# Keys and values of two groups by seven products in one PSUM bank, in an attention layer on one core

## The chip, the cores and the metric

The kernel runs on one core of a Trainium2 chip. The metric is the time of one execution on the device in microseconds; smaller is better. A core has a matrix engine (TensorE, in profiles PE, with its weight loads as PEld), a vector engine (VectorE, DVE), an activation engine (ScalarE, ACT), a general engine (GpSimd, POOL) and a queue engine (SyncE, SP) that issues most of the DMAs. Each has its own in-order queue, and they wait for each other by semaphores. Matrix products land in PSUM, which has eight banks of 2 KB in each of 128 partitions; everything else lies in SBUF.

## The reference

All numbers are float32. For x of 2 batches x 512 tokens x 512 features, with 32 query heads in 8 groups (four query heads share one key head and one value head of 128 columns):

```python
q = x @ Wq + bq;  k = x @ Wk + bk;  v = x @ Wv + bv        # 4096, 1024 and 1024 columns
q, k = rope(q, pos), rope(k, pos)
scores = einsum("bgrsd,bgtd->bgrst", q, k) / sqrt(128)     # masked to t <= s
ctx = einsum("bgrst,bgtd->bgrsd", softmax(scores), v)
x = layernorm(x + ctx @ Wo + bo)
# then a dense layer with four low-rank experts, mixed by a softmaxed router
y = x @ W_base.T + b_base + sum_e alpha_e * (x @ A_e.T @ B_e.T) * 2
out = layernorm(x + y)
```

Four experts of sixteen are active; their rows of lora_A, lora_B and router_W are gathered by index.

## The kernel before

**Units, parts, slots.** A *unit* is one group of one batch: 16 units. Units 0 to 11 go through groups 0 to 5 with both batches each; the last four are (6,0), (7,0), (6,1), (7,1). A unit has four *parts* (128 query tokens of its four heads) and a part four *slots*; a slot is the softmax of 128 rows (32 tokens x 4 heads) over the keys up to the diagonal, so its width grows from 32 to 512 columns within a unit. `slot(T)` writes down the work of slot T for all engines by hand: the schedule is manual, so each engine executes in the order in which the code issues. `put(n, f)` appends f to the end of slot n.

**The softmax chain.** In slot T: `score(T)` on PE (L488), then `masked_max(T-1)` on DVE (L496), `exponentials(T-1)` and `normalise(T-3)` on ACT (L503, L511), `blocks_transposed(T-4)` on DVE (L519, L521). When four slots are done, `blocks_out` writes the part's weights to DRAM and `blocks_in` reads them back transposed as pT (L529, L537, on SP). `weigh` (L544) multiplies pT with v on PE, 12 slots after the part's first score and later, and `context_out` (L550) copies the bank to SBUF on ACT. Score banks are two, the context bank is one.

**Projections.** x is held transposed as xT. Keys: four products of 128x512 per unit (`k_mm`, `proj_mm`, L355), one in each of the first four slots of the unit before. Then `k_rope` in three steps on DVE (L368, L371, L375) and one on POOL (L376) straight from the bank. Values: `v_mm` (L342) makes a tile of 128 tokens x 256 columns, both groups of a pair, by four products; `v_out` (L347) adds bv, broadcast over the partitions, on DVE. Two such tiles fall into each unit.

Queries are already made by Strassen's scheme in Winograd's form, two heads at a time and a batch halved into twice 256 tokens: seven products of half the size instead of eight (`q_products`, `product`, L429, two matmuls of 256 columns each). Sums of the weights are made on POOL (`w_sums`, `strassen_sums`, L416 to L419), sums of x once per batch on DVE (`x_sums`, xs). The products go to two banks, qx and qy; after certain products ACT copies the running sum of qx (`q_copy`, L457, L460), and DVE adds qy to the copy (`q_sum`, L467 to L472).

Wo is multiplied in the same way (`wo_products`, `ctx_sums` on POOL, `wo_sums` on DVE, L568), in slots that begin 21 after a unit's first (`wo_from`); its results are added to x on DVE (`wo_adds`, L601).

**What sets the order of loads.** SP takes its DMAs in order, and one that waits holds the next. `load_q`, `load_k`, `load_wv` and `load_wo` are put into slots by hand; each waits until its buffer is free.

Of the kernel before, what the change touches and what calls it, by code (L numbers as in the profile page):

```python
# [29 lines left out]
def postln_layer_kernel(  # L30
# [84 lines left out]
    rope_sb = const.tile([P, 2, S], F32, name="rope_sb")  # L115
    bqkT = const.tile([P, H + G], F32, name="bqkT")

# [43 lines left out]
    def load_wv(gg):  # L161
        wv_g = wts.tile([P, KC, VN], F32, tag="wv_g", name=f"wv_{gg}", bufs=1)
        nc.sync.dma_start(out=wv_g, in_=Wv[:, ts(gg, VN)].rearrange("(c p) n -> p c n", p=P))
        bv_g = wts.tile([P, VN], F32, tag="bv_g", name=f"bv_{gg}")
        nc.sync.dma_start(out=bv_g, in_=bv[ts(gg, VN)].partition_broadcast(P))
        wvs[gg] = wv_g, bv_g

# [20 lines left out]

    bqk = setup.tile([H + G, D], F32, name="bqk")
    nc.scalar.dma_start(out=bqk[:H, :], in_=bq.rearrange("(h d) -> h d", d=D))  # L190
    nc.scalar.dma_start(out=bqk[H:, :], in_=bk.rearrange("(h d) -> h d", d=D))
    for t in range(TPB):
# [25 lines left out]
    nc.gpsimd.iota(lane, pattern=[[0, 1]], base=0, channel_multiplier=1)  # L218
    a_act = setup.tile([EAR, HID], F32, name="a_act")
    r_act = setup.tile([EA, HID], F32, name="r_act")  # L220
    rb_act = setup.tile([EA, 1], F32, name="rb_act")
# [41 lines left out]
    def gather_experts():  # L263
        gather(a_act, lora_A.rearrange("e r n -> (e r) n"), idx["a"])
        gather(r_act, router_W, idx["e"])
        for a in range(EA):
            gather(b_act[:, a, :], lora_B.rearrange("e (p j) r -> (e p) (j r)", j=BJ), idx["b"][:, a : a + 1])
# [11 lines left out]
    def lora_weights(step):  # L279
        if step == 0:  # L280
            ta = ps_wo.tile([P, KC, EAR], F32, tag="wx", name="ta")
            for c in range(KC):
                nc.tensor.transpose(ta[:, c, :], a_act[:, ts(c, P)], ident[:EAR, :EAR])
            nc.vector.tensor_copy(arT[:, :, :EAR], ta)
            nc.vector.tensor_copy(b_jar, b_act.rearrange("p a (j r) -> p j a r", r=RK))
        elif step == 1:
            tr = ps_wo.tile([P, KC, EA], F32, tag="wx", name="tr")
            for c in range(KC):
                nc.tensor.transpose(tr[:, c, :], r_act[:, ts(c, P)], ident[:EA, :EA])
            nc.vector.tensor_copy(arT[:, :, EAR:], tr)  # L290
        else:

            tbm = ps_wo.tile([EAR, BJ, P], F32, tag="wx", name="tbm")
            for j in range(BJ):
                nc.tensor.transpose(tbm[:, j, :], b_jar[:, j, :, :].rearrange("p a r -> p (a r)"), ident)
            nc.vector.tensor_copy(bmT[:EAR, :].rearrange("k (p j) -> k j p", j=BJ), tbm)
# [41 lines left out]
    def v_mm(gg, t, c, pool, tag):  # L338

        if c == 0:  # L340
            psq["v", gg, t] = pool.tile([P, VN], F32, tag=tag, name="pv")
        nc.tensor.matmul(  # L342
            psq["v", gg, t], lhsT=xT[:, c, ts(t, P)], rhs=wvs[gg][0][:, c, :], start=(c == 0), stop=(c == KC - 1))

    def v_out(gg, t):
        v_sb[gg, t] = work.tile([P, VN], F32, tag="v", name=f"v_{gg}_{t}", bufs=11)
        nc.vector.tensor_tensor(v_sb[gg, t], psq["v", gg, t], wvs[gg][1], ALU.add)  # L347

# [9 lines left out]
    def rope_step(key, bias_col, part, dst):  # L358
# [8 lines left out]
        if part == 0:  # L367
            nc.vector.scalar_tensor_tensor(  # L368
                t2[lo, :], q[hi, :], b_ap[hi, :], rope_sb[hi, 1, :], ALU.add, ALU.mult)
        elif part == 1:  # L370
            nc.vector.scalar_tensor_tensor(  # L371
                t2[hi, :], q[lo, :], b_ap[lo, :], rope_sb[lo, 1, :], ALU.add, ALU.mult)
        else:
            t1 = proj.tile([P, S], F32, tag="raw0", name="t1", bufs=2) if key in in_psum else q
            nc.vector.scalar_tensor_tensor(t1, q, b_ap, rope_sb[:, 0, :], ALU.add, ALU.mult)  # L375
            nc.gpsimd.tensor_tensor(  # L376
                dst, t1[:].rearrange("p (n s) -> p n s", s=BLK), t2[:].rearrange("p (n s) -> p n s", s=BLK), ALU.add)

    def k_mm(u, c):
        g, b = unit(u)  # L380
        proj_mm(("k", u), ps_k, "k", wqk["k", g], slice(0, D), b, c)

    def k_rope(u, part):
        if part == 0:
            kT[u] = work.tile([P, UNIT, BLK], F32, tag="kT", name=f"kT_{u}")
        rope_step(("k", u), H + unit(u)[0], part, kT[u])
# [46 lines left out]
    def q_products(u, k, step):  # L433
# [18 lines left out]
        else:  # L452
            product(halves[key]["qy"], w[:, 2], x2[:, :, TH:], False)

    def q_copy(u, k, name):
        if name == "c21":
            nc.scalar.copy(psq["q", u, 2 * k + 1][:, :TH], halves[u, k]["qx"])  # L457
            return
        part = halves[u, k][name] = proj.tile([P, TH], F32, tag=name, name=name)
        nc.scalar.copy(part, halves[u, k]["qx"])  # L460

    def q_sum(u, k, step):
        key = u, k
        z = halves[key]
        if step == 0:
            psq["q", u, 2 * k] = proj.tile([P, S], F32, tag="raw0", name="q0", bufs=2)
            nc.vector.tensor_tensor(psq["q", u, 2 * k][:, :TH], z["qy"], z["p1"], ALU.add)  # L467
        elif step == 2:
            psq["q", u, 2 * k + 1] = proj.tile([P, S], F32, tag="raw1", name="q1")
            nc.vector.tensor_tensor(psq["q", u, 2 * k + 1][:, TH:], z["qy"], z["u3"], ALU.add)  # L470
        else:
            nc.vector.tensor_tensor(psq["q", u, 2 * k][:, TH:], z["qy"], z["u2"], ALU.add)  # L472

# [65 lines left out]
    def weigh(p, j):  # L539
        u, i = parts[p]  # L540
        g, b = unit(u)
        if j == 0:
            psc[p] = ps_ctx.tile([P, R, P], F32, tag="ctx", name="pc")
        nc.tensor.matmul(  # L544
            psc[p], lhsT=v_sb[g // VG, b * TPB + j][:, ts(g % VG, D)], rhs=pT[p][:, :, ts(j, P)],
            start=(j == 0), stop=(j == i))

    def context_out(p):
        ctxT[p] = work.tile([P, R, P], F32, tag="ctxT", name=f"ctxT_{p}", bufs=3)
        nc.scalar.copy(ctxT[p], psc[p])  # L550

# [241 lines left out]
    put(T_BEGIN, gather_experts)  # L793
    for n, gg, t in [(2 * t - 1, 0, TPB + t) for t in range(TPB)] + [(2 * t + 11, 1, t) for t in range(3)]:
        put(n, lambda gg=gg, t=t: v_tile(gg, t, ps_wo, "wx"))
        put(n + 1, lambda gg=gg, t=t: v_out(gg, t))
# [3 lines left out]
    for k in range(3):  # L800
        put(-4 + k, lambda k=k: prior_weights(k))
        put(12 + 2 * k, lambda k=k: lora_weights(k))
    put(1, lambda: load_q(1, 1))
    put(6, lambda: load_wv(1))
    put(9, lambda: load_wo(1))
    for t in range(NT):
# [7 lines left out]
    for m, (n, k) in enumerate(pairs):  # L814
        if n:
            put(q_from(set_units(n)[0], k) - 9, lambda n=n, k=k: w_sums(n, k))
        if m > 3:
            before, k_before = pairs[m - 3]
            put(q_from(set_units(before)[-1], k_before) + 8, lambda n=n, k=k: load_q(n, k))
    for g in range(2, G):  # L820
        put(2 * UNIT * (g - 1) - 24, lambda g=g: load_k(g))
    for gg in range(2, G // VG):
        put(4 * UNIT * (gg - 1) + 30, lambda gg=gg: load_wv(gg))

# [5 lines left out]
    for n in range(NSETS - 2):  # L830
        for k in range(4):
            put(wo_from(set_units(n)[0]) - 1 + k, lambda n=n, k=k: wo_sums(n, k))

# [15 lines left out]
    def slot(T):  # L849
# [13 lines left out]
        uk, l = divmod(T + UNIT, UNIT)  # L863
        if 0 < uk < NU and l < KC:
            k_mm(uk, l)

        gv, tv = divmod(2 * (uk - 3) + (l >= 11), NT)
        gv += 1
        new_v = 0 < gv < G // VG and (gv > 1 or tv >= 3)
        if new_v and l in (7, 8, 11, 12):  # L870
            for c in range(2):
                v_mm(gv, tv, 2 * (l in (8, 12)) + c, ps_k, "k")
        kw, sw = divmod(T - LAG_WO, 8)
# [13 lines left out]
        if now and step in (0, 2, 4, 6):  # L887
            q_copy(uq, kq, ("p1", "u2", "u3", "c21")[step // 2])
        for part, j in weigh_at.get(T - 1, ()):
            if j == parts[part][1]:  # L890
# [11 lines left out]
        if now and step in (1, 5, 7):  # L902
            q_sum(uq, kq, {1: 0, 5: 2, 7: 3}[step])
        if 0 <= T - 2 < T_END:
# [15 lines left out]
        if 0 <= r < R and part < 3:  # L920
            q_rope(1, r, part)
        if 0 < uk < NU and l in (KC, KC + 1, KC + 2):
            k_rope(uk, l - KC)
        if new_v and l in (10, 14):
            v_out(gv, tv)
        if plain and step_o:
# [12 lines left out]
    for t in range(TPB):  # L939
        transpose_token_tile(xT[:, :, ts(t, P)], x_sb[:, t, :], *spare[t], copies[t % 2])  # L940
    tb = ps_sc.tile([P, H + G], F32, tag="sc", name="tb")
    nc.tensor.transpose(tb, bqk, ident[: H + G, : H + G])
    nc.vector.tensor_copy(bqkT, tb)
# [22 lines left out]
    for T in range(T_BEGIN, T_SETUP):  # L966
        slot(T)
    setup_stack.close()
    T_PROJ = T_END - 19
    for T in range(T_SETUP, T_PROJ):  # L970
# [178 lines left out]
```

## Time and profile before

| | before |
|---|---|
| median of 3 runs | 838.86 us (838.44 to 840.26) |
| the profiled execution, its own time | 839.75 us |
| its span, first to last instruction | 838.0 us |
| PE busy | 825.9 us (99%), 3201 matmul records |
| DVE busy | 595.6 us (71%) |
| ACT busy | 354.3 us (42%) |
| POOL busy | 290.1 us (35%) |
| granted PE clock, mean | 0.996 |

A busy time is that of an engine's instructions; a wait names the engine and line that waited and what it waited for. Matmuls overlap in PE's pipeline, so the mean duration of one record is longer than the distance between two. A float32 matmul of the program has two records, a transpose one. "The chain" is the sequence of work that ended last, followed back from the end.

### The profile page before, as it was taken

The numbers are of one execution on the slowest core, as the hardware profiler recorded it, in microseconds if no ns is written. First come the engines' busy times: TensorE is split into PE (matmuls) and PEld (weight loads), VectorE is DVE, ScalarE is ACT, GpSimd is POOL, SyncE is SP. The second block draws the span as 40 slices with busy tenths as digits, with TensorE's granted clock in tenths as the row PEclk, the third lists the DMA queues.
The fourth block names the chain that finished last, engine by engine and source line by source line (L and its number), as shares of the span: only waits on it lengthen the run. The fifth ranks groups of instructions, "written<-read, shape, count | busy, mean of one in ns | idle before, by whom it ended". The sixth has DMA issues, their size and how long they took to land.

```text
span 838.0 us, 10735 instructions
## 1 busy us (share of the span) xinstructions
PE 825.9 (99%) x3201; PEld 583.9 (70%) x3201; DVE 595.6 (71%) x1964; ACT 354.3 (42%) x1002; POOL 290.1 (35%) x318
## 2 busy tenths in 40 slices
PE   8999999999999999999999999999999999999996
PEld 5566677777777777777777777777777776655574
DVE  5468977787767967686767866687767878964535
ACT  1225454534434444444434343444435344663133
POOL 6463344233322334232332334334333523300022
PEclk9999999999999999999999999999999999999998
DMA  9126536364553556263543557274544536574211
GB/s 289 39 63 190 157 83 194 103 177 123 151 148 102 166 152 194 62 175 115 151 138 105 172 148 193 61 204 143 152 125 126 177 90 199 163 247 118 63 39 63
DMA packets 84971, 116.47 MB, mean 139 GB/s; under 512 B 6581, under 2 KB 64797, under 8 KB 82866
## 3 DMA queue, kind: packets, MB, share of 16 engines
q1 hardware_dynamic: 84258, 115.50, 48.1%
q0 software_dynamic: 448, 0.14, 0.2%
q8 instruction: 25, 0.41, 0.2%
q14 instruction: 32, 0.26, 0.1%
q10 hardware_dynamic: 208, 0.15, 0.1%
HBM read 71.73 MB, written 44.04 MB: 138 GB/s over the span
## 4 chain that ended last, share of the span: by engine, by line
PE 90%; DVE 4%; DMA 2%; ACT 1%; issue 1%; POOL 1%; SPq 0%; DVEq 0%; POOLq 0%
PE pc L544 16%; PE sc L488 13%; PE qx L429 11%; PE wx L429 11%; PE pp L355 9%; PE qy L429 8%; PE wy L429 8%; PE pv L342 6%; PE py L686 3%; PE po L615 3%; DMA pT<-db 1%; PE tp L274 1%; PE py L731 1%; DMA db<-zt 1%; DMA x_sb<-_attn_hidden_states_dram 1%
## 5 line engine op out<-in xcount | busy, mean ns | idle before, releaser
L503 ACT ACTIVATE p<-sc,nmax 128x288 f32<-128x288 f32 (+15 forms) x256 | 124.4, 486 | 253.0 <-DVE nmax L496 207.5
L496 DVE CUSTOM_DVE_ANT_0 sc<-sc,maskw 128x288 f32<-128x288 f32 (+15 forms) x256 | 114.1, 446 | 154.5 <-PE sc L488 151.7
L544 PE MATMUL pc<-pT,v 128*128 128x512 f32 x320 | 165.5, 599 | 0.6 <-DMA pT<-db 0.6
L488 PE MATMUL sc<-kT,qT 128*128 128x160 f32 (+15 forms) x512 | 162.0, 398 | 1.2 <-ACT p L503 1.1
L376 POOL TENSOR_TENSOR qT<-q,t 128x512 f32<-128x512 f32 x56 | 71.0, 1268 | 188.8 <-DVE q L375 188.8
L511 ACT ACTIVATE p<-p,den 128x288 f32<-128x288 f32 (+15 forms) x256 | 133.4, 522 | 0.1
L488 PEld LDWEIGHTS sc<-kT,qT 128*128 128x128 f32 x512 | 96.7, 190 | 30.3 <-issue 14.3
L416 POOL TENSOR_TENSOR cs<-ctxT 128x256 f32<-128x256 f32 x28 | 26.5, 948 | 196.2 <-PE wy L429 109.5
L550 ACT COPY ctxT<-pc 128x512 f32<-128x512 f32 x64 | 37.5, 586 | 124.9 <-PE pc L544 124.9
L519 DVE STREAM_TRANSPOSE zt<-p 128x128 f32<-128x128 f32 (+2 forms) x192 | 81.6, 425 | 0.0
L544 PEld LDWEIGHTS pc<-pT,v 128*128 128x128 f32 x320 | 57.0, 190 | 19.7 <-issue 5.4
L355 PE MATMUL pp<-xT,wk 128*128 128x512 f32 x128 | 65.0, 593 | 0.5 <-ACT xT L275 0.5
L342 PE MATMUL pv<-wv,xT 128*128 128x256 f32 x256 | 63.6, 379 | 0.0
L429 PE MATMUL wx<-wo,ctxT 128*128 128x256 f32 x224 | 57.7, 380 | 0.4 <-DVE den L507 0.4
L429 PE MATMUL qx<-xs,wq 128*128 128x256 f32 x224 | 58.0, 381 | 0.0
L342 PEld LDWEIGHTS pv<-wv,xT 128*128 128x128 f32 x256 | 48.5, 190 | 13.4 <-issue 6.9
L521 DVE STREAM_TRANSPOSE zt<-p 128x32 f32<-128x32 f32 (+3 forms) x256 | 57.4, 224 | 0.0
L429 PEld LDWEIGHTS qx<-xs,wq 128*128 128x128 f32 x224 | 41.4, 190 | 22.3 <-issue 16.0
L429 PEld LDWEIGHTS wx<-wo,ctxT 128*128 128x128 f32 x224 | 42.4, 190 | 13.5 <-issue 7.7
L503 ACT ACTIVATION_READ_ACCUMULATOR p<-sc,nmax 128x1 f32 x256 | 49.9, 195 | 0.0
L601 DVE TENSOR_TENSOR x_sb<-wx,x_sb 128x256 f32<-128x256 f32 x112 | 46.9, 419 | 0.0
L368 DVE SCALAR_TENSOR_TENSOR t<-q,bqkT,rope_sb 64x512 f32<-64x512 f32 x56 | 43.0, 768 | 1.3
(190 smaller groups left out, 1362.9 us busy)
## 6 DMA issues: line engine op xcount, KB each, us to landing
db<-zt SPq DMA_DIRECT2D x64, 256.0 KB, 4.1
pT<-db SPq DMA_DIRECT2D x16, 1024.0 KB, 4.8
db<-zt SPq DMA_DIRECT2D x64, 192.0 KB, 3.2
pT<-db SPq DMA_DIRECT2D x16, 768.0 KB, 4.5
wq<-in_L_attn_Wq_dram SPq DMA_DIRECT2D x20, 512.0 KB, 4.7
wo<-in_L_attn_Wo_dram SPq DMA_DIRECT2D x10, 1024.0 KB, 7.6
db<-zt SPq DMA_DIRECT2D x64, 128.0 KB, 2.4
pT<-db SPq DMA_DIRECT2D x16, 512.0 KB, 4.1
```

Source lines behind the costliest of these rows:

```text
L342: nc.tensor.matmul(psq["v", gg, t], lhsT=xT[:, c, ts(t, P)], rhs=wvs[gg][0][:, c, :], start=(c == 0), stop=(c == KC - 1))
L355: nc.tensor.matmul(psq[key], lhsT=wt[:, c, cols], rhs=xT[:, c, ts(b, S)], start=(c == 0), stop=(c == KC - 1))
L376: nc.gpsimd.tensor_tensor(dst, t1[:].rearrange("p (n s) -> p n s", s=BLK), t2[:].rearrange("p (n s) -> p n s", s=BLK), ALU.add)
L429: nc.tensor.matmul(ps, lhsT=wt[:, c, :], rhs=xt[:, c, :], start=start and c == 0, stop=c == CH - 1, skip_group_check=True)
L488: nc.tensor.matmul(sc[s][:, :w], lhsT=qT[u][:, i * QB + n].rearrange("p r s -> p (r s)"), rhs=kT[u][:].rearrange("p n s -> p (n s)")[:, :w ...
L496: nc.vector.tensor_tensor_reduce(sc[s][:, :w], sc[s][:, :w], maskw[:, S - w :], -SCALE, -MASKED, ALU.add, ALU.min, nmax[s])
L503: nc.scalar.activation(ptile[s][:, :w], sc[s][:, :w], AF.Exp, bias=nmax[s], scale=-1.0, accum_out=rden[s])
L511: nc.scalar.activation(ptile[s][:, :w], ptile[s][:, :w], AF.Copy, scale=rden[s])
L519: nc.vector.transpose(z[:, :, last - i : last, n, :].rearrange("p q j s -> p j q s"), ptile[s][:, : i * P])
L521: nc.vector.transpose(z[:, : n + 1, last, n, :], ptile[s][:, i * P : w])
L544: nc.tensor.matmul(psc[p], lhsT=v_sb[g // VG, b * TPB + j][:, ts(g % VG, D)], rhs=pT[p][:, :, ts(j, P)], start=(j == 0), stop=(j == i))
L601: nc.vector.tensor_tensor(into, pw[k, bank], into, ALU.add)
```

## The change

Four things are changed together.

1. *Keys and values of groups 2 to 7 by seven products.* Two groups of a pair take the place of the two heads in the query scheme. A block (kind, pair, batch) has one frame of 16 slots; the frames of a pair are key batch 0, key batch 1, value batch 0, value batch 1. Both running sums x and y lie in one bank (`ps_k`, 2 x 256 columns). ACT copies four times, DVE adds three times, in place. A key product is two matmuls of 256 columns; a value product is four of 128, since the tokens are the stationary side. Keys of units 0 to 3, values of pair 0 and of pair 1's batch 0 stay plain. Seven slots of a frame hold a product, seven others a copy or an add.
2. *The bias of v* is no longer added to v. Since the softmax sums to one, it is added to the context on its way out of PSUM (L550's copy becomes an activation with bias). bv is loaded once as eight rows beside bq and bk. Plain value tiles are copied by ACT.
3. *Other slots.* The key ropes move from slots 4, 5, 6 of a unit to 11, 13, 14 (3, 5, 6 for the last); the four Wo sums from -1, 0, 1, 2 to 0, 1, 1, 3 after `wo_from`; `load_q` two slots, the second `load_wo` eight slots later; key loads come in pairs. Query copies go directly to their place, and the adds work in place.
4. *Gathered rows* of lora_A and router_W lie in one tile and are transposed together.

The diff, cut to its core:

```diff
-    bqkT = const.tile([P, H + G], F32, name="bqkT")
+    NBIAS = H + 2 * G
+    bqkT = const.tile([P, NBIAS], F32, name="bqkT")
...
-        bv_g = wts.tile([P, VN], F32, tag="bv_g", name=f"bv_{gg}")
-        nc.sync.dma_start(out=bv_g, in_=bv[ts(gg, VN)].partition_broadcast(P))
...
+    nc.scalar.dma_start(out=bqk[H + G :, :], in_=bv.rearrange("(h d) -> h d", d=D))
...
     def v_out(gg, t):
-        v_sb[gg, t] = work.tile([P, VN], F32, tag="v", name=f"v_{gg}_{t}", bufs=11)
-        nc.vector.tensor_tensor(v_sb[gg, t], psq["v", gg, t], wvs[gg][1], ALU.add)
+        nc.scalar.copy(v_of(gg, t // TPB)[:, t % TPB, :], psq["v", gg, t])
...
+    KV_STEPS = {0: 1, 2: 2, 4: 6, 6: 7, 8: 4, 10: 5, 12: 3}
+    KV_OUT = {1: "p1", 3: "c11", 5: "u2", 7: "u3", 9: "c21", 11: "c22", 13: "c12"}
+    KV_ON_ACT = ("p1", "u2", "u3", "c21")
...
+    def kv_sums(kind, p):
+        w = kvs[kind, p] = late["pool"].tile([P, 3, CH, D], F32, tag="kvs", name=f"kvs_{kind}_{p}")
+        strassen_sums(
+            nc.gpsimd, *(kv_block(kind, p, h, c) for h in range(2) for c in range(2)), *(w[:, m] for m in range(3)))
+
+    def kv_products(kind, p, b, step):
+        key = kind, p, b
+        x1, x2 = (xT[:, CH * c : CH * (c + 1), ts(b, S)] for c in range(2))
+        if step == 1:
+            halves[key] = ps_k.tile([P, 2, TH], F32, tag="k", name=f"{kind}x")
+        half, w, xt = {
+            1: (0, (0, 0), x1[:, :, :TH]), 2: (1, (0, 1), x2[:, :, :TH]), 6: (0, 1, xs[:, b, 1]),
+            7: (0, (1, 0), xs[:, b, 2]), 4: (0, (1, 1), xs[:, b, 3]), 5: (1, 0, xs[:, b, 0]),
+            3: (1, 2, x2[:, :, TH:]),
+        }[step]
...
+        if kind == "k":
+            product(ps, w, xt, first)
+        else:
+            for t in range(2):
+                for c in range(CH):
+                    nc.tensor.matmul(
+                        ps[:, ts(t, P)], lhsT=xt[:, c, ts(t, P)], rhs=w[:, c, :],
+                        start=first and t == c == 0, stop=c == CH - 1, skip_group_check=True)
...
+        if name in KV_ON_ACT:
+            nc.scalar.copy(into, x)
+        else:
+            nc.vector.tensor_tensor(into, y, into, ALU.add)
...
     def context_out(p):
         ctxT[p] = work.tile([P, R, P], F32, tag="ctxT", name=f"ctxT_{p}", bufs=3)
-        nc.scalar.copy(ctxT[p], psc[p])
+        col = H + G + unit(parts[p][0])[0]
+        nc.scalar.activation(ctxT[p], psc[p], AF.Identity, bias=bqkT[:, col : col + 1])
...
-    put(9, lambda: load_wo(1))
+    put(17, lambda: load_wo(1))
...
-            put(q_from(set_units(before)[-1], k_before) + 8, lambda n=n, k=k: load_q(n, k))
-    for g in range(2, G):
-        put(2 * UNIT * (g - 1) - 24, lambda g=g: load_k(g))
-    for gg in range(2, G // VG):
-        put(4 * UNIT * (gg - 1) + 30, lambda gg=gg: load_wv(gg))
+            put(q_from(set_units(before)[-1], k_before) + 10, lambda n=n, k=k: load_q(n, k))
+    PLAIN_K = 2 * B
+    KV_FROM = 8
+    PERIOD = VG * B * UNIT
+    for p in range(1, G // VG):
+        at = PERIOD * p
+        put(13 if p == 1 else at - PERIOD + 9, lambda p=p: load_k(VG * p))
+        put(37 if p == 1 else at - PERIOD + 13, lambda p=p: load_k(VG * p + 1))
+        put(40 if p == 1 else at - 2 * UNIT + 3, lambda p=p: kv_sums("k", p))
+        if p > 1:
+            put(at - PERIOD + 37, lambda p=p: load_wv(p))
+        put(at + (UNIT if p == 1 else 0) + 3, lambda p=p: kv_sums("v", p))
...
-            put(wo_from(set_units(n)[0]) - 1 + k, lambda n=n, k=k: wo_sums(n, k))
+            put(wo_from(set_units(n)[0]) + (0, 1, 1, 3)[k], lambda n=n, k=k: wo_sums(n, k))
...
-        new_v = 0 < gv < G // VG and (gv > 1 or tv >= 3)
-        if new_v and l in (7, 8, 11, 12):
-            for c in range(2):
-                v_mm(gv, tv, 2 * (l in (8, 12)) + c, ps_k, "k")
+        kv, o = kv_at(T)
+        if kv and o in KV_STEPS:
+            kv_products(*kv, KV_STEPS[o])
...
+        if kv and KV_OUT.get(o) in KV_ON_ACT:
+            kv_out(*kv, KV_OUT[o])
...
+        if kv and o in KV_OUT and KV_OUT[o] not in KV_ON_ACT:
+            kv_out(*kv, KV_OUT[o])
...
-        if 0 < uk < NU and l in (KC, KC + 1, KC + 2):
-            k_rope(uk, l - KC)
-        if new_v and l in (10, 14):
-            v_out(gv, tv)
+        k_slots = (4, 5, 6) if uk < PLAIN_K else (11, 13, 14) if uk < NU - 1 else (3, 5, 6)
+        if 0 < uk < NU and l in k_slots:
+            k_rope(uk, k_slots.index(l))
```

## The prediction, made before the changed kernel ran

> **What bounds the kernel now.** I read first the table of seven stretches of the span. Its columns are the stretch, then busy time and instructions of PE, PEld, DVE, ACT and POOL, the granted clock, the DMA share and GB/s.
>
> ```profile
> 0.00:62.00 62.00, 59.29 (x204) 36.54 (x205) 33.98 (x84) 12.52 (x31) 36.70 (x48) 1.00 0.41 129
> 62.00:105.00 43.00, 42.05 (x174) 29.95 (x173) 38.23 (x122) 20.57 (x62) 17.24 (x16) 1.00 0.60 174
> 105.00:383.00 278.00, 278.00 (x1102) 204.21 (x1101) 208.21 (x691) 123.98 (x364) 95.49 (x102) 1.00 0.51 143
> 431.00:690.00 259.00, 259.00 (x1026) 190.39 (x1026) 192.90 (x633) 113.34 (x328) 93.94 (x103) 1.00 0.50 139
> 690.00:745.00 55.00, 54.03 (x195) 33.83 (x193) 44.37 (x153) 30.74 (x80) 15.19 (x23) 1.00 0.65 198
> ```
>
> In the body PE is busy 278.00 of 278.00 us and 259.00 of 259.00, DVE about 75%, ACT 44%, POOL 35%. So there a removed matmul should be removed time. From 62 to 105 us DVE is busy 89% and from 690 to 745 us 81%: a saving in those two stretches may not be paid out.
>
> Second, the waits. Those of PE sum to 6.6 us in the whole span, and from 45 to 690 us only two are over the listing's floor (the first two lines below: waiter, awaited, total us, times, longest). The other lines show who follows whom.
>
> ```profile
> PE pc L544 <- DMA pT<-db: 0.6, 1, 0.6
> PE qy L429 <- DVE q L470: 0.3, 1, 0.3
> DVE sc L496 <- PE sc L488: 151.7, 137, 2.3
> PEld qy L429 <- DVE q L470: 4.9, 8, 1.2
> POOL cs L416 <- PE wy L429: 109.5, 14, 8.8
> ```
>
> DVE waits for a score 137 times out of 256 slots, 1.1 us each: it catches up with PE in every second slot.
>
> Third, the rate of a matmul. The mean duration in the groups (593 ns for 512 columns, 379 for 256) includes the pipeline, and consecutive matmuls overlap, so I take the rate from the chain of waits (start us, us, what, xcount) and from starts in the timeline.
>
> ```profile
> 18.67 1.73 PE pv L342 x8
> 20.40 3.43 PE pp L355 x8
> 800.75 1.33 PE tp L274 x12
> 814.77 1.70 PE zl L696 x16
> ```
>
> ```profile
> 224.53 0.38 PE L488 MATMUL sc<-kT,qT 128*128 128x128 f32 x2
> 224.75 1.03 PE L429 MATMUL wy<-wo,cs 128*128 128x256 f32 x4
> ```
>
> A record of 512 columns takes 3.43/8 = 0.429 us, one of 256 columns 1.73/8 = 0.216, one of 128 columns (a transpose) 1.33/12 = 0.111. The 16 to 20 columns of L696, each with a full 128x128 weight load, still take 1.70/16 = 0.106: that is the pace of weight loads, although one load lasts 190 ns. A plain matmul has two records (16 units of 4 key products are x128 in the page), a transpose one.
>
> **The change part by part.**
>
> *Keys.* Three pairs of groups, two batches: six blocks. A block was two units of 4 products: 16 records x 0.429 = 6.86 us. It becomes 7 products of 2 matmuls with 256 columns: 28 x 0.216 = 6.05. Saved 0.81, six times: 4.9 us.
>
> *Values.* The first pair's batch 0 stays plain, so five blocks. A block was 4 token tiles x 4 chunks of 256 columns: 32 x 0.216 = 6.91. It becomes 7 x 4 matmuls of only 128 columns: 56 x 0.111 = 6.22. Saved 0.69, five times: 3.5 us. No row has this product, so bounds: the score of 128 columns is a plain matmul of the same shape and its pair takes 0.22 us in the timeline (starts 224.53 to 224.75), which gives 56 x 0.110 = 6.16; the other end is a record that waits out its whole 190 ns load, 56 x 0.190 = 10.64. I take 0.111, since both the transposes and the score, nearest in shape, run at it.
>
> The Trainium skill, "TensorE: Matmul & The Clock Gate", section "Back-to-back issue gap", speaks against this part: it has 81 ns a matmul at 128 columns against 131 at 512, so a narrow one would be dear. Scaled to 0.429 us, an estimate from that page makes a narrow record 0.265, a block 14.9 us and the value part 39.7 us slower; the trace's 0.111 says otherwise.
>
> *Expert rows.* One transpose of 36 rows in place of one of 32 and one of 4: four L289 records and their bank change go, 0.4 us of PE.
>
> Sum of PE work removed: 4.9 + 3.5 + 0.4 = 8.8 us.
>
> *What the other engines get.* DVE loses 32 adds of v (409 ns) and gains 11 blocks x 3 adds of the q kind (414): +0.6 us. ACT gains 44 copies and the 12 plain value tiles, 56 x 372 ns = 21 us on 354; the bias of v rides on the context eviction, a COPY of 586 ns that becomes an activation of the same shape (bounds: 366 ns, a copy half as wide, and 726, the widest L511 activate; I take 586, because L511 and L503 show 687 to 726 for the same 512 columns and the copy is the nearest form: with 726 ACT gets 9 us more and is still busy only 46%). POOL gains six sets of four sums, by the ws rows 729+907+764+756 = 3.2 us each: 19 us on 290. All of this lies beside PE in the body; if that cover failed, each would cost its own length in the slot where it is late. Ropes of keys keep their number and read SBUF in place of PSUM (768+747+710 against 755+744+729: nothing).
>
> *New hand-overs.* x and y of a block share one bank, and the program as built makes PE wait for the reader of either half: six waits per block (after p1, c11, u2, u3, c21, c22), 66 in all. Each reader stands in the slot after its product and the next product one slot later, like L467 to L472 now. The row for this is PEld qy <- DVE q: 8 of 84 such sums are waited for, 0.6 us each, of which PE lost 0.3 us altogether. c11 and c22 follow directly on the maximum of their slot, so they are earlier than those; I price the 66 at zero, bounds 0 and 66 x 0.6 = 40 us. Queued behind a late one would be that slot's Wo products, score and context on PE.
>
> The Trainium skill, "PSUM — Partial Sum Buffer", section "PSUM bank collisions raise a hardware error", wants guards by bank and not by address, so none of these waits could be dropped by finer tracking. No run here shows a collision.
>
> *Sums on POOL.* Four of the six sets reuse a buffer whose last product is one slot later, so POOL stands until PE has done it, and the context sums queue behind 3.2 us of work. They start today when PE frees cs (the wait of 109.5 us), nearly three slots of 2.96 us (47.3/16, below) before wx needs the second of them, and that one is there after 948+742 ns. Delayed by 3 us they still make it: I take zero, at worst 3 us x 4.
>
> *Sums of Wo.* L568 moves so that the second sum (1.02 us) comes one slot ahead of wx instead of two, beside 0.67 us in the same slot; the ropes of keys leave those slots. In the body I take zero: DVE has 25% free. At 690 to 745 us it is part of the chain already (1.14, 1.02, 0.60 us pieces), and there the last block adds two sums of 0.41 us to DVE just where PE stops being the bound. I take 0.7 us back for this, bounds 0 and 2.
>
> *Loads.* Four broadcasts of bv (128 KB, 6.6 us each) go, one small load on ACT's queue comes; its issue (0.4 to 0.6 us by its two neighbours) ends long before 6.8 us, when PE starts on the fourth x tile. The second Wo load leaves the slot of the first pT, which took 6.8 us against a median of 4.4 and cost PE the 0.6 us above; it now stands beside the third and fourth. Wq loads go two slots later on SP, K loads are regrouped; SP's queue already waits 380 us for DVE, and the sums that read the weights stand five slots or more behind. Three value evictions leave DVE in the stretch from 62 to 105 us: 3 x 0.41 = 1.2 us off an engine at 89%. I credit 0.4, bounds -1 (pT delayed later) and +1.5.
>
> Total: -8.8 + 0.7 - 0.4 = -8.5 us. The profiled execution took 839.75 us (span 838.0), so 831.25 for it; the median of the runs, 838.86, lies 0.9 below, and from it the sum gives 830.4 us.
>
> **The rivals.**
>
> *Part of it lost, 835 us.* PE becomes short enough that DVE, with 3 adds per block in tight places, sets the pace of some slots, or POOL's late context sums stop wx. Four POOL events at 1 us and some 0.5 us from the tail: about 4.5 us given back. For it: DVE's 89 and 81%. Against: DVE's 137 waits for PE.
>
> *Slower, 848 us.* The hand-overs within one bank are not covered: at 8.5/66 = 0.13 us each they eat the gain, at 0.27 us the time is 838.86 - 8.5 + 66 x 0.27 = 848. For it: a wait over DVE happens already, and there will be a reader between any two products of a block. Against: PE has lost only 0.3 us to 84 similar ones.
>
> *Slower, 852 us.* Narrow value products at 190 ns: 5 x (10.64 - 6.22) = 22 us more, 830.4 + 22. For it only the load's duration; against it the two rows at 0.11 us.
>
> *It does nothing, 838.9 us:* PE's removed work reappears as waits for the softmax chain. DVE's waits for PE speak against it.
>
> **How the numbers follow.** My case gets 0.73, part lost 0.14, no effect 0.03, the bank 0.07, narrow products 0.03. Runs of this kernel spread by 0.2%, so that is what counts as no change. Faster 0.87, same 0.03, slower 0.10. Own range of my case: 828 (all early waits gone, nothing lost in the tail) to 832.5; with the partly lost case up to 834.
>
> **What would show it.** PE busy for all of the body; records of the narrow product at starts 0.11 us apart; a unit of 16 slots 0.7 to 0.8 us shorter than 47.3 (today the 32-column scores that open two units start at 357.20 and 404.51 us); no PE wait for kx or vx over 0.3 us; ACT busy near 375 us, POOL near 309, DVE unchanged. Wrong if PE waits for ACT or DVE after a kx or vx product, or if narrow records come 0.19 us apart.

## The result, and the profile after

The median of six runs went from 838.75 to 831.4 us: 0.991 of the time before, with a 95% interval of 0.9892 to 0.9927. That is 7.35 us less; the forecast was 830.4, between 828 and 834.

The first view is the same table of stretches, of the kernel after (columns as before: busy time and instructions of PE, PEld, DVE, ACT, POOL, then granted clock, DMA share, GB/s). The span ends about 10 us earlier, so the last two stretches are moved by 10 us.

```profile
0.00:62.00 62.00, 59.98 (x206) 36.94 (x207) 31.63 (x76) 15.52 (x39) 36.71 (x48) 1.00 0.40 127
62.00:105.00 43.00, 42.95 (x177) 31.31 (x176) 36.42 (x116) 22.05 (x66) 16.56 (x16) 1.00 0.60 171
105.00:383.00 278.00, 278.00 (x1164) 211.67 (x1163) 215.02 (x709) 133.82 (x387) 105.67 (x114) 1.00 0.50 142
...
431.00:680.00 249.00, 249.00 (x1120) 193.48 (x1119) 192.90 (x623) 120.86 (x345) 104.08 (x111) 1.00 0.50 143
680.00:735.00 55.00, 53.50 (x205) 34.56 (x204) 46.04 (x154) 30.50 (x80) 15.71 (x23) 1.00 0.64 195
```

PE is still busy for all of the body, 278.00 of 278.00 and 249.00 of 249.00, although every other engine has more to do there: the removed matmul time is removed time. The stretch from 62 to 105 us has PE at 42.95 of 43.00 where it had 42.05. Only from 680 to 735 us did PE lose something: it idles 1.50 us of 55 where it idled 0.97.

The timeline of PE after (start, us, what) holds the starts by which the matmul rate and the length of a unit are read.

```profile
279.26 1.05 PE L512 MATMUL vx<-wv,xT 128*128 128x128 f32 x8
280.15 1.03 PE L434 MATMUL wy<-wt,cs 128*128 128x256 f32 x4
...
352.88 0.30 PE L546 MATMUL sc<-kT,qT 128*128 128x32 f32 x2
399.35 0.30 PE L546 MATMUL sc<-kT,qT 128*128 128x32 f32 x2
445.97 0.30 PE L546 MATMUL sc<-kT,qT 128*128 128x32 f32 x2
492.66 0.30 PE L546 MATMUL sc<-kT,qT 128*128 128x32 f32 x2
```

Eight narrow records fill 280.15 - 279.26 = 0.89 us, so one takes 0.111. The unit from 352.88 to 399.35 us holds all 28 records of a key block and lasts 46.47 us; the one from 445.97 to 492.66 holds all 56 of a value block and lasts 46.69. Before, each lasted 47.31 us. They are 0.84 and 0.62 shorter.

The third view is the waits of PE after (waiter, awaited, total us, times, longest).

```profile
PE sc L546 <- ACT p L561: 1.7, 3, 1.1
PE tz L785 <- DVE zs L776: 1.3, 1, 1.3
PE idle L1016 <- DVE maskw L175: 1.2, 1, 1.2
PE wy L434 <- DVE x_sb L660: 0.9, 2, 0.7
PE pp L355 <- ACT xT L276: 0.5, 1, 0.5
PE tp L275 <- ACT xT L276: 0.2, 1, 0.2
```

That is the whole list: no kx or vx is in it, so the 66 new hand-overs within a bank cost PE nothing that shows. The early wait for pT (0.6 us) is gone, and the wait of a Wo product for DVE (0.2 us before) has grown to 0.9.

**Why the two profiles differ by more than the medians.** The profiled executions took 839.75 and 829.5 us, 10.25 apart; the latter is the fastest of its six runs. The chain of waits of both names a part of it. In each, the same twelve matmuls near the end (start, us, what) follow one another without a gap:

```profile
817.53 4.65 PE py L686 x12
```

```profile
808.45 2.97 PE py L745 x12
```

The first line is of before, the second of after. The work is the same, but the first took 1.68 us longer: for 3.4 us of it PE was granted half its clock, as this stretch of before shows (columns as above).

```profile
817.50:820.90 3.40, 3.40 (x9) 2.57 (x9) 2.72 (x13) 1.97 (x4) 0.00 (x0) 0.50 0.00 0
```

The execution profiled in after has no such stretch before its last 3 us. This belongs to the execution and not to the kernel alone: the changed kernel run again below (`after_again`) does these twelve matmuls in 2.97 us too, but has 0.50 from 820.6 to 824.0 us. Of the fourteen profiles of this document, the eight with a mean clock of 0.996 or 0.997 have such a stretch of 3.4 us between 809 and 824 us, the six with 0.998 or 0.999 have none. A list of times holds executions of both kinds, and its median depends on the mixture. PE's first wait for x differs too: 0.8 us in before, under the listing's floor after, 0.2 to 1.5 in runs below. So this pair of profiles does not measure the change; the medians do, within the spread that this mixture gives them.

### The profile page after: what moved, and what is told of

Its sections match the earlier page's. It is cut to its first block, busy times and chain, and to the rows that moved or that the text cites. A ratio compares the mean times of both kernels' runs of the same rounds, so it can differ in the third digit from the quotient of the medians.

```text
span 827.4 us, 11161 instructions
## 1 busy us (share of the span) xinstructions
PE 816.1 (99%) x3389; PEld 597.5 (72%) x3389; DVE 602.3 (73%) x1964; ACT 378.8 (46%) x1058; POOL 313.7 (38%) x342
## 4 chain that ended last, share of the span: by engine, by line
PE 93%; DVE 4%; ACT 2%; issue 1%; POOL 1%; DVEq 0%; POOLq 0%
PE pc L602 16%; PE sc L546 14%; PE qx L434 11%; PE wx L434 11%; PE qy L434 9%; PE wy L434 8%; PE pp L355 5%; PE kx L434 4%; PE vx L512 4%; PE py L745 3%; PE po L674 3%; PE pv L338 3%; PE tp L275 1%; PE py L790 1%; DVE sc L554 0%
## 5 line engine op out<-in xcount | busy, mean ns | idle before, releaser
L376 POOL TENSOR_TENSOR qT<-q,t 128x512 f32<-128x512 f32 x56 | 76.9, 1372 | 179.9 <-DVE q L375 179.9
L609 ACT ACTIVATE ctxT<-pc,bqkT 128x512 f32<-128x512 f32 x64 | 44.0, 687 | 116.4 <-PE pc L602 116.4
L421 POOL TENSOR_TENSOR cs<-ctxT 128x256 f32<-128x256 f32 x28 | 22.2, 794 | 157.8 <-PE wy L434 93.7
L470 ACT COPY q<-qx 128x256 f32<-128x256 f32 x112 | 41.3, 369 | 36.6 <-PE qx L434 36.6
L368 DVE SCALAR_TENSOR_TENSOR t<-q,bqkT,rope_sb 64x512 f32<-64x512 f32 x56 | 45.0, 804 | 1.5
L701 POOL TENSOR_SCALAR y<-y,mv_f,rstd_f 128x512 f32<-128x512 f32 x4 | 8.5, 2129 | 94.2 <-DVE rstd_f L698 94.2
L371 DVE SCALAR_TENSOR_TENSOR t<-q,bqkT,rope_sb 64x512 f32<-64x512 f32 x56 | 42.2, 754 | 1.3
```

The costliest lines, as they stand in the source:

```text
L368: nc.vector.scalar_tensor_tensor(t2[lo, :], q[hi, :], b_ap[hi, :], rope_sb[hi, 1, :], ALU.add, ALU.mult)
L376: nc.gpsimd.tensor_tensor(dst, t1[:, :].rearrange("p (n s) -> p n s", s=BLK), t2[:, :].rearrange("p (n s) -> p n s", s=BLK), ALU.add)
L609: nc.scalar.activation(ctxT[p], psc[p], AF.Identity, bias=bqkT[:, col : col + 1])
```

## The experiments

The runs were made in three groups, each on one chip beside the kernel before (838.73, 839.17 and 838.47 us there). Times are medians and ratios are to the kernel before.

**The kernel unchanged, and its two parts taken apart.** `after_again` has no edit.

> The changed kernel once more, as the base for the other three. Theory 1 (PE is the bound, so every removed matmul is removed time) and theory 2 (a good part of the gain comes from the other edits: loads, bias, slots) both expect 830 to 832 us and the kernel before at about 838.8.

`keys_only` makes the values of all pairs plainly, in the same frames (the diff is cut to its core here and below):

```diff
-        if kv and o in KV_STEPS:
+        plain_v = kv and kv[0] == "v"
+        if plain_v and o % 4 < 2:
+            for c in range(2):
+                v_mm(kv[1], kv[2] * TPB + o // 4, 2 * (o % 4) + c, ps_k, "k")
+        elif kv and not plain_v and o in KV_STEPS:
...
-        put(at + (UNIT if p == 1 else 0) + 3, lambda p=p: kv_sums("v", p))
```

> Values plain again, four tiles of 4 x 256 columns in each block's own 16 slots with a copy by ACT, no sums of Wv on POOL; all else as in the changed kernel. Theory 1: 5 blocks x (32 x 0.216 - 56 x 0.111) = 3.5 us slower than the changed kernel, about 835. Theory 2: about 832 to 833. Theory 3 (narrow products and their hand-overs cost as much as they save, all of the gain is that of the keys): 831.4 or below.

`values_only` makes the keys plainly, with one copy of the finished bank on ACT:

```diff
+        plain_k = kv and kv[0] == "k"
+        if plain_k and o in (0, 1, 2, 3, 6, 7, 8, 9):
+            k_mm(units.index((VG * kv[1] + o // 6, kv[2])), o % 6)
...
-        put(40 if p == 1 else at - 2 * UNIT + 3, lambda p=p: kv_sums("k", p))
```

> Keys of groups 2 to 7 plain again, eight products of 512 columns in each block's 16 slots, the bank copied to SBUF by ACT, no sums of Wk on POOL; all else as in the changed kernel. Theory 1: 6 x 0.81 = 4.9 us slower than the changed kernel, about 836.3. Theory 2: 833 to 834. Theory 3: about 838, since then the keys hold all of the gain.

`both_plain` does both, so that only the rest of the change is left: the bias of v, the slots, the loads, the gathered rows. (ACT still copies values and keys out of PSUM, and the ropes still read those keys from SBUF.)

> Both of these at once: what is left of the change are the bias on the context, the joined gathers, the loads and the slots. Theory 1: 8.4 us slower than the changed kernel, about 839.8, thus no better than the kernel before. Theory 2: 834 to 836. Theory 3: as theory 1 for the sum, but with all of it in the keys.

| | us | ratio | interval | mean of the runs with a clock of 0.998 or more | first to last slot in the profile |
|---|---|---|---|---|---|
| after_again | 831.09 | 0.9914 | 0.9889 to 0.9939 | 830.20 (3 runs) | 717.16 |
| keys_only | 833.62 | 0.9935 | 0.9913 to 0.9957 | 831.97 (2) | 719.70 |
| values_only | 835.87 | 0.9958 | 0.9945 to 0.9972 | 834.54 (5) | 722.03 |
| both_plain | 838.88 | 0.9993 | 0.9978 to 1.0008 | 836.82 (5) | 724.64 |
| before | 838.73 | 1 | | 837.93 (11) | 725.93 |

The last column is the distance from the start of the first slot's maximum on DVE to that of the last. It ends before the stretch of half clock and begins after the waits for x. These are the two starts in before and in `after_again`:

```profile
45.70 0.20 DVE L496 CUSTOM_DVE_ANT_0 sc<-sc,maskw 128x32 f32<-128x32 f32 x1 [0.34 <-PE sc L488]
771.63 0.40 DVE L496 CUSTOM_DVE_ANT_0 sc<-sc,maskw 128x256 f32<-128x256 f32 x1
```

```profile
45.83 0.20 DVE L554 CUSTOM_DVE_ANT_0 sc<-sc,maskw 128x32 f32<-128x32 f32 x1 [2.00 <-PE sc L546]
762.99 0.40 DVE L554 CUSTOM_DVE_ANT_0 sc<-sc,maskw 128x256 f32<-128x256 f32 x1
```

The two parts add up. By the medians, keys are worth 838.88 - 833.62 = 5.3 us without the values and 835.87 - 831.09 = 4.8 with them; values 838.88 - 835.87 = 3.0 without the keys and 833.62 - 831.09 = 2.5 with them. Together that is 7.8 us. From first to last slot, keys are worth 4.9 us both ways and values 2.6 and 2.5.

The rest of the change looks worthless by the medians: with both parts undone the time is that of before, with an interval that reaches from 1.8 us faster to 0.7 slower. But the median of `both_plain` falls among its seven runs with a clock under 0.998. In the runs with 0.998 or more it is 1.1 us faster than before, and from first to last slot 1.3 us shorter. So the rest is worth about 1 us, which the medians hide.

Where the values lose a little shows in the table of stretches. This is the stretch of `keys_only` that answers to 680 to 735 us of after, of the same columns:

```profile
680.00:735.00 55.00, 54.05 (x207) 36.00 (x206) 47.22 (x159) 29.74 (x82) 15.68 (x23) 1.00 0.64 187
```

PE idles 0.95 us of it, as before; with the values by seven products it idles 1.50. The wait of a Wo product for DVE is 0.2 us in `keys_only` as before, against 0.9 after. So the last value block takes back some 0.55 us here.

**The bank's hand-overs without the spare slot.** `tight` puts the seven products into seven slots in a row, with each reader in the slot of its product:

```diff
-    KV_STEPS = {0: 1, 2: 2, 4: 6, 6: 7, 8: 4, 10: 5, 12: 3}
-    KV_OUT = {1: "p1", 3: "c11", 5: "u2", 7: "u3", 9: "c21", 11: "c22", 13: "c12"}
+    KV_STEPS = {0: 1, 1: 2, 2: 6, 3: 7, 4: 4, 5: 5, 6: 3}
+    KV_OUT = {0: "p1", 1: "c11", 2: "u2", 3: "u3", 4: "c21", 5: "c22", 6: "c12"}
```

> The seven products of a block stand in slots 0 to 6 of its frame, each read by ACT or DVE in its own slot and followed by the next product in the next slot: the spare slot between product and reader is gone, the work is the same. If the hand-overs in the one bank are free only because of that slot (theory 1), PE now waits for ACT or DVE at kx and vx, by 0.1 to 0.2 us on the mean of 66, so 838 to 845 us. If the engines follow so closely that the slot was never needed: 831 to 832. If hand-overs cost something of their own in any case, PE waits are there in the changed kernel too, which its profile denies.

It took 832.33 us, 0.9911 (0.9883 to 0.9939) of before, where `loads_back`, below, took 831.27 on the same chip: no difference that the intervals can tell. The waits of PE and its weight loads:

```profile
PE sc L546 <- ACT p L561: 1.6, 3, 1.1
...
PEld kx L434 <- ACT q L470: 1.4, 6, 0.2
PEld vx L512 <- ACT q L470: 1.2, 5, 0.2
```

PE waits for the softmax as it did, and still no wait for kx or vx is in the list, whose shortest entries are 0.2 us. The weight loads now do wait, 11 times for at most 0.2 us, and nothing of that reaches a matmul in the list.

**The loads put back.** `loads_back` undoes the later slots of the loads:

```diff
-    put(17, lambda: load_wo(1))
+    put(9, lambda: load_wo(1))
...
-            put(q_from(set_units(before)[-1], k_before) + 10, lambda n=n, k=k: load_q(n, k))
+            put(q_from(set_units(before)[-1], k_before) + 8, lambda n=n, k=k: load_q(n, k))
```

> The second load of Wo back from slot 17 to 9 and the loads of Wq two slots earlier, as in the kernel before; all else as in the changed kernel. If the moved loads were worth something, PE waits for the first pT again (0.6 us in the kernel before) and the time is 831.5 to 832.5; if they only go along, 831.1 as the changed kernel. It can't explain more than 1 us.

831.27 us, 0.9908 (0.988 to 0.9937): the same. PE's wait for the first pT does not come back, so the moved Wo load was not what removed it. What did stays open; the broadcast of bv, which the change takes off SP's queue just before, is a candidate that no run put back.

**The end of the queries' work.** `ropes_early` moves the key rope of the last unit one unit earlier, out of the stretch where DVE is busiest:

```diff
-        k_slots = (4, 5, 6) if uk < PLAIN_K else (11, 13, 14) if uk < NU - 1 else (3, 5, 6)
-        if 0 < uk < NU and l in k_slots:
+        k_slots = (4, 5, 6) if uk < PLAIN_K else (11, 13, 14)
+        if 0 < uk < NU - 1 and l in k_slots:
...
+        if uk == NU - 2 and l in (3, 5, 6):
+            k_rope(NU - 1, (3, 5, 6).index(l))
```

> The rope of the last unit's keys moves from slots 227, 229, 230 to 211, 213, 214, where DVE waits for PE; nothing else. The changed kernel's value block of the last pair gives back 1 us between slots 216 and 232, where DVE is the bound. If that is DVE's backlog, 2.9 us leave it there, PE's waits for x_sb and p between 690 and 705 us go and the time is 829.5 to 830.3. If the end is held by the softmax chain through ACT and POOL: 831.

`ropes_and_pool` also gives two of the Wo sums of that stretch to POOL:

```diff
-        nc.vector.tensor_tensor(
+        (nc.gpsimd if n == NSETS - 3 and step > 1 else nc.vector).tensor_tensor(
```

> As the one before, and the last two of the four Wo sums of the last set are done by POOL in place of DVE (0.7 and 1.7 us of DVE in the profile). If DVE is still the bound there: 829 to 829.8. If POOL's sums slow DVE down when both run, as the 1.75 us of a sum that usually takes 0.67 suggests, no better than the kernel without it, or worse by up to 1 us.

829.26 us, 0.9879 (0.9857 to 0.9901), and 830.29 us, 0.9896 (0.9871 to 0.9921). The first is 2.0 us under `loads_back` on the same chip, with intervals that overlap; the second adds nothing to it. The stretch of `ropes_early`:

```profile
680.00:735.00 55.00, 54.60 (x214) 36.18 (x213) 44.44 (x157) 31.75 (x84) 13.21 (x22) 1.00 0.69 204
```

PE idles 0.40 us of it against 1.50 after, and DVE has 1.6 us less to do: the idle time there was DVE's doing. The rope is not free in its new place, though. From 431 to 680 us PE now idles 0.38 us, in one wait that the kernel after does not have:

```profile
PE qy L434 <- DVE q L474: 0.4, 1, 0.4
```

Of the 1.1 us some 0.7 are left. From first to last slot `ropes_early` is 1.1 us shorter than after (715.96 against 717.07). The 2.0 us of the medians are partly the mixture: five of the six runs of `ropes_early` had a clock of 0.998 or more, two of the four of `loads_back`, and these differ by 1.0 us (828.94 and 829.93).

**Smaller suspects.** `two_sum_buffers` gives the weight sums of keys and values two buffers (`bufs=2`), so that POOL need not stand until PE has done with the first.

> The sums of Wk and Wv get two buffers, so that POOL no longer stands for up to 4.9 us until PE has done the last product of the block before (19.2 us of waits in the changed kernel's profile). If POOL's late sums hold up wx or the ropes anywhere: 829 to 830.5. If POOL has that time (theory 1): 831, with the waits gone.

`wo_sums_back` returns the sums of Wo to their old slots, `(0, 1, 1, 3)[k]` to `(-1, 0, 1, 2)[k]`.

> The four sums of Wo back in slots -1, 0, 1, 2 after the set's first Wo slot; all else as in the changed kernel. In the body DVE now has the key ropes out of those slots, so theory 1 expects no difference there; in the tail the sums come a slot earlier but meet the same backlog: 830.8 to 831.6. If the move was needed to keep PE running, PE waits for DVE at x_sb or p rise by more than 2 us: 833 and more.

`no_bias` makes the context eviction a plain copy again (`nc.scalar.copy(ctxT[p], psc[p])`); it leaves out the bias of v.

> The bias of v is left out altogether: the context leaves PSUM by a plain copy. ACT gets 64 x (687 - 586) = 6.5 us less. If ACT is covered everywhere: 831. If the longer eviction holds back the Wo products or the softmax in the tail: 829.5 to 830.5.

They took 829.96 us (0.9913, 0.9885 to 0.9941), 831.36 (0.9912, 0.989 to 0.9935) and 831.35 (0.9924, 0.9905 to 0.9943): none differs from after. What POOL waited for in the kernel after (here the first fence) and in `two_sum_buffers` (the second) shows that the buffer did what it should:

```profile
POOL cs L421 <- PE wy L434: 93.7, 14, 8.7
...
POOL kvs_k L421 <- PE vx L512: 9.7, 2, 4.9
POOL kvs_v L421 <- PE kx L434: 9.5, 2, 4.7
```

```profile
POOL cs L421 <- PE wy L434: 103.3, 18, 8.7
```

POOL's four waits of up to 4.9 us were there, as predicted, and vanish with the second buffer; half of their time goes into the wait for cs. The time stays, so the context sums behind them were never late for PE.

**A cost that nobody had counted.** The groups of after (line, engine, operation, out<-in, shape, count | busy us, mean ns) have the second step of the key rope in two forms:

```profile
L371 DVE SCALAR_TENSOR_TENSOR t<-kT,bqkT,rope_sb 64x512 f32<-64x512 f32 x12 | 14.2, 1185 | 0.2
L371 DVE SCALAR_TENSOR_TENSOR t<-pp,bqkT,rope_sb 64x512 f32<-64x512 f32 x12 | 8.8, 744 | 0.2
```

With the keys read from SBUF (kT) it takes 1185 ns, with the keys read from PSUM (pp) 744. The timeline of after around one of them shows what POOL did at that time:

```profile
296.31 0.72 POOL L424 TENSOR_TENSOR ctxT<-ctxT,ctxT 128x256 f32<-128x256 f32 x1
...
296.40 1.18 DVE L371 SCALAR_TENSOR_TENSOR t<-kT,bqkT,rope_sb 64x512 f32<-64x512 f32 x1
...
296.99 1.71 POOL L376 TENSOR_TENSOR qT<-q,t 128x512 f32<-128x512 f32 x1
```

DVE's step starts 0.09 us after a sum on POOL and ends 0.55 us after it; POOL's next instruction starts within DVE's step and takes 1.71 us, where the mean of this form before was 1.27. `ropes_quiet` is `ropes_early` with the steps in slots 8, 9, 10 (0, 1, 2 for the last unit), where POOL does not make the sums of the context:

```diff
-        k_slots = (4, 5, 6) if uk < PLAIN_K else (11, 13, 14)
+        k_slots = (4, 5, 6) if uk < PLAIN_K else (8, 9, 10)
...
-        if uk == NU - 2 and l in (3, 5, 6):
-            k_rope(NU - 1, (3, 5, 6).index(l))
+        if uk == NU - 2 and l in (0, 1, 2):
+            k_rope(NU - 1, (0, 1, 2).index(l))
```

> The ropes of all keys by seven products move from slots 11, 13, 14 of a unit to 8, 9, 10, where POOL does not make the sums of the context, and those of the last unit to slots 208, 209, 210. If it is POOL's work at the same time that stretches the second step of a key rope to 1185 ns (744 from PSUM), the step falls to 750 to 800 ns; if it is the source in SBUF, it stays near 1185. For the time, as in the kernel with the last rope early: 829 to 830, since the body's DVE is covered.

The same group in `ropes_quiet`:

```profile
L371 DVE SCALAR_TENSOR_TENSOR t<-kT,bqkT,rope_sb 64x512 f32<-64x512 f32 x12 | 8.9, 745 | 0.4
```

Still from SBUF, it is back at 745 ns. So the 440 ns are no price of SBUF as such but of meeting POOL. POOL is not idle in the new place either, as the timeline of `ropes_quiet` shows around one of the twelve:

```profile
284.77 0.75 DVE L371 SCALAR_TENSOR_TENSOR t<-kT,bqkT,rope_sb 64x512 f32<-64x512 f32 x1
284.88 1.77 POOL L376 TENSOR_TENSOR qT<-q,t 128x512 f32<-128x512 f32 x1 [8.75 <-ACT p L569]
```

Here POOL starts 0.11 us after DVE, in all twelve, and it is POOL that takes longer: 1.77 us where 1.27 is usual. In the kernel after, POOL's sum had started together with DVE's step or up to 0.12 us before it, and DVE paid. The kind of POOL's instruction does not decide it: in the kernel after, a sum (L423) that starts 0.13 us after an L371 at 268.02 us takes 1.21 us itself and leaves DVE at 0.74. So it counts which of the two starts first, and not only whether both run.

In time it is worth little: 829.44 us, 0.99 (0.9881 to 0.9918), not to be told from `ropes_early` (0.9879), and between it and after the intervals overlap. From first to last slot `ropes_quiet` takes 715.05 us, 2.0 less than after and 0.9 less than `ropes_early`, in one profile each; after and `after_again` differ by 0.1 there. These two have the lowest medians of all kernels run. That they beat the kernel after is likely by these distances and the table of stretches, and not proven by the times.

## Why the prediction was right, point by point

**Keys, 4.9 us.** Measured 4.8 to 5.3 by the medians and 4.9 from first to last slot. The unit with a whole key block is 0.84 us shorter, and the row rates give the same: a unit before held half a key block and half a value block, (6.86 + 6.91)/2 = 6.89 us, and now 6.05.

**Values, 3.5 us, less 0.7 in the tail.** Measured 2.5 to 3.0 by the medians and 2.5 to 2.6 from first to last slot, against 2.8. The narrow record takes 0.111 us, the value taken from the transposes and the scores; the unit with a value block is 0.62 us shorter, where 6.89 - 6.22 gives 0.67. The tail's share is what the stretch of `keys_only` shows: 0.55 us more idle time of PE with the value blocks, at the place named.

The estimate from the Trainium skill, "TensorE: Matmul & The Clock Gate", section "Back-to-back issue gap", was 0.265 us for this record; the trace has 0.111, and the measurement decides.

**Hand-overs, zero, with 40 us as the far bound.** No wait of PE for kx or vx is listed in any run, also with the spare slot taken away. The rival of 848 us falls with it, the rival of 852 us with the 0.111 us, and the rival of no effect with PE's 278.00 of 278.00.

**POOL's late sums, zero.** The waits existed (19.2 us of POOL in four, each longer than the 3 us taken as the worst) and cost nothing that shows: `two_sum_buffers`, without them, is not clearly faster, and no shorter from first to last slot (717.35 us).

**Expert rows and the credit for loads and evictions, 0.4 each.** About right, though the medians do not show it: `both_plain` holds all of it and is 1.3 us shorter than before from first to last slot. The parts themselves are seen: PE's record count rose by 188, which is 6 x 12 + 5 x 24 - 4, so the four expert records are gone; the wait for pT is gone; PE idles 0.9 us less from 62 to 105 us. About 0.3 us are lost again behind the last slot: with the stretch of half clock in it, the way from there to the end takes 66.4 us in before and 66.6 to 66.7 in the changed kernels. Why stays open. The reason given for the pT wait (the moved Wo load) was wrong: with the load put back, the wait stays away.

**The sum, 8.5 us.** The medians gave 7.35, with an interval from 6.1 to 9.1. From first to last slot the change is worth 725.93 - 717.07 = 8.9 us. Of this, 0.3 are lost behind the last slot, and another 0.3 outside the span, which no term of the sum held: the runs take 2.07 us more than their span in `after_again` and 1.79 in the kernel before beside it. Why is open too. The runs with a clock of 0.998 or more differ by 837.93 - 830.20 = 7.7 us, with three runs on one side.

**Ropes of keys from SBUF in place of PSUM, "nothing".** This step failed. DVE's busy time rose by 6.7 us (595.6 to 602.3) and not by 0.6; twelve times 0.44 us of L371 is 5.3 of it. Most of it was hidden in the body by DVE's free quarter. What it cost the changed kernel was not measured alone; taking the ropes away from POOL's sums is worth 0.9 us from first to last slot (`ropes_early` against `ropes_quiet`, one profile each). The rows that the prediction priced it by were query ropes, which with the same two inputs in SBUF took 747 ns on average: the form of the instruction was the same, its company was not. The first step of those same ropes already showed it before, behind a mean of 768 ns. Three of the 56 took 1.08 to 1.10 us, each with a POOL instruction begun 0.2 to 0.7 us earlier (minimum, median and maximum follow the count):

```profile
L368 DVE SCALAR_TENSOR_TENSOR t<-q,bqkT,rope_sb x56: 749/750/1099, 80.0 to 714.4; 64x512 f32<-64x512 f32 x56
```

The Trainium skill, "SBUF — State Buffer", section "Who interferes with whom", has the rule: a DVE instruction with two inputs in SBUF contends with a GpSimd instruction that reads SBUF, and the one that issues first holds up the other. The rows above agree with it on both sides: where POOL started first, DVE took 1185 ns against 745; where DVE started first, POOL took 1.71 and 1.77 us against 1.27.

**ACT and POOL.** ACT is at 378.8 us where 375 was predicted. The group of the context eviction after:

```profile
L609 ACT ACTIVATE ctxT<-pc,bqkT 128x512 f32<-128x512 f32 x64 | 44.0, 687 | 116.4 <-PE pc L602 116.4
```

687 ns against the 586 taken; it lies inside the bounds, nearer to 726, and 64 x 101 ns = 6.5 us are all hidden, since without them (`no_bias`) the time is the same. The Trainium skill, "ScalarE: Activation LUTs", section "What ACT_TABLE_LOAD costs", has about 93 ns for a bias that is a [128,1] operand; the row's 101 is near it. POOL is at 313.7 where 309 was predicted.

## What to carry to other kernels

Where one engine is busy for all of a stretch, removed records are worth their spacing in the timeline, and the sum over blocks is the gain; the mean durations in the groups (593 and 379 ns) would have made a key block dearer, 28 x 0.379 = 10.6 us in place of 16 x 0.593 = 9.5. Undoing the two halves of a change one by one shows whether they add up, and undoing both shows what the rest was worth. Differences of 1 us are hard to read from medians of a few executions of which some have 3.4 us of half clock and some have not; the distance between two fixed points of the traces shows them, here 1.3 us where the medians had nothing. A row prices an operation together with what ran beside it: before taking a row for a moved instruction, look at its longest as well as at its mean, and in the timeline at what the other engines do in the new place and which starts first.

## What the runs showed of the hardware that was not expected

- A DVE instruction of 64x512 with two SBUF inputs took 1185 ns on average where a POOL instruction that reads SBUF had started with it or up to 0.12 us before it. Where POOL's started 0.11 us after it, DVE took 745 ns and POOL's 128x512 sum 1.77 us instead of 1.27. With one input in PSUM the DVE instruction took 744 ns.
- Two accumulators in one PSUM bank, read by ACT and DVE between the products, held up PE by no listed wait in 66 hand-overs, with a slot between product and next product or without.
- In some executions PE was granted half its clock for 3.4 us near the end, in others of the same kernel not: twelve identical matmuls took 4.65 us in one and 2.97 in another, and the way from the last slot to the end 66.65 us in `after_again` and 65.00 in after.
